# Where K's token term is added: in the copies of M1 and M7 instead of the last addition

## The chip, the core and the metric

The kernel runs on one core of a Trainium2 chip. The metric is the device time of one execution in microseconds; the median of the runs is compared. The engines are named as in the profile: PE is TensorE (matrix products), PEld its weight loads, DVE is VectorE, ACT is ScalarE, POOL is GpSimd and SP is SyncE, which issues most DMAs. SBUF is the working memory of 128 partitions, PSUM the memory into which PE writes, here used as 8 banks of 512 float32 values a partition.

## The reference

Attention over x of shape (8, 512, 512) with 16 heads of 32 columns; one token per batch is projected by the same weights and added to every row of Q and K.

```python
Q = _split_heads(x @ Wq.T + bq)
K = _split_heads(x @ Wk.T + bk)
V = _split_heads(x @ Wv.T + bv)
tQ = _split_heads(tokens @ Wq.T + bq)
tK = _split_heads(tokens @ Wk.T + bk)
cQ = Q + tQ
cK = K + tK
scores = jnp.einsum('bhqd,bhkd->bhqk', cQ, cK) / jnp.sqrt(jnp.float32(HEAD_DIM))
attn = jax.nn.softmax(scores, axis=-1)
out = jnp.einsum('bhqk,bhkd->bhqd', attn, V)
...
x = x + out
```

(The last line stands for the reference's merging of the heads and its addition to x.) Per batch and output column, the token's part of K and both biases are one number: the token term.

## The kernel before

**Groups and thirds.** The 16 heads of a batch make 4 groups of 4 heads (one head to 32 partitions), so there are T = 32 groups t = b * 4 + g. The main loop (`thirds`, line 1156) makes one round for every group and is written by hand as the order of every engine's queue: a manual schedule, in which each engine works through its instructions in the order in which the program issues them and semaphores hold an instruction until its inputs are there and its output is free. A round has three parts, i = 0, 1, 2. In it the row maxima of the scores of the next groups are found (`row_scores` L641 on PE, `one_max` L593 and `row_max_of` L650 on DVE), exponentials are taken (`denominators` L701 and `rest_leaves` L799 on ACT), the weighted sums over V are formed (`times_v_half` L840 on PE), and one piece of the next batch's Q, K or V is projected in each part.

**Projections by seven products.** Q, K and V of a batch are made block-wise in a Strassen-like scheme: for two groups at a time (u = 0 or 1), seven products M1 to M7 of 256 columns replace the block products (`product`, PE at L462). A pair tile holds the upper group (c1 with its second half c12) and the lower group (c2 with its second half c22). For K the work comes in two pieces:

- "k first" (`first_by_others` with `mixed` None): PE makes M1 and M7 into one bank (`one_`), M6 and half of M2 into another (`two_`). DVE copies M1 and M7 to c2 and c22 (L530), adds M1 twice to `two_` to give c1 and c12 (L531), and POOL adds c12 to c22 (L533).
- "k other" (`other_products` with `bias` true): PE makes M4, M5, the other half of M2 and M3 into two banks. DVE adds M5 to c12 (L555), then forms c2 from the bank, c22 and the token term of the lower group (`plus`, L487, group 1), then c1 from the bank, c1 and the token term of the upper group (`plus`, L487, group 0).

Over the run k first and k other occur 14 times each in the main loop, k first in part 2 of every second round and k other in part 1 of the rounds between. Q's "other" goes through the same L487; V has no token term. The first batch's groups take other paths (`project_qk`, `first_products`, and `other_products` with `bias` false).

**The token terms.** `tok` (line 926) holds one float32 per partition for Q or K, group and batch; Q's entries are written by DVE and K's by POOL (`condition_end`, L949), near the start. `bias2` holds twice the biases that go into it.

**Banks.** The eight PSUM banks are handed around by `begin`, `released` and `banks`. After k first the banks of the products go last into the next round's row maxima; after k other the next part's row scores (L641) write into them as well. So PE's L641 waits for the DVE instruction that has read such a bank last.

**The kept exponentials.** Half of a group's exponentials are kept, turned by DVE (`turn_kept`, L660) and swapped between partitions by DMAs issued by SP and POOL (`swap_kept`, L682) until the next round's L840 reads them. The other transfers of the loop load x (L172 and L190) and store results (L917). ACT, DVE and POOL never work on two of their instructions out of order.

Of the kernel before, what the change touches and what calls it, by code (L numbers as in the profile page):

```python
# [9 lines left out]
F32 = mybir.dt.float32  # L10
BF16 = mybir.dt.bfloat16
AF = mybir.ActivationFunctionType
ALU = mybir.AluOpType
# [4 lines left out]
def kernel(  # L18
# [38 lines left out]
    nc = tc.nc  # L57
    P = 128
    B, S, D = x.shape
# [14 lines left out]
    const = ctx.enter_context(tc.tile_pool(name="const", bufs=1))  # L74
# [41 lines left out]
    def banks(i, n=1):  # L116

        row = row_of[0] or [at_end[j] for j in TURNS[turn[0]]]
        j = row[i]
        if n == 1:  # L120
            return psum[:, j, :]
        k = row[i + 1]
        return psum[:, j : k + 1 : k - j, :]
# [273 lines left out]
    def pair_of(t, n):  # L397

        if (n, t // 2) not in pairs:
            pairs[n, t // 2] = qkp.tile([P, 2, S], F32, tag=n, name=f"{n}T_{t // 2}")  # L400
        return pairs[n, t // 2]

    def project_qk_part(t, n, cc, pt, at=slice(0, S)):
        b, g = divmod(t, G)
        nc.tensor.matmul(
            pt[:, at],
            wT[n][:, cc, g * P : (g + 1) * P],
            xT[b][:, cc, at],
            start=(cc == 0),
            stop=(cc == NC - 1),  # L410
        )

    def project_qk_end(t, n, pt):
        b, g = divmod(t, G)
        o = pair_of(t, n)[:, t % 2, :]
        add = tok[:, "qk".index(n), g, b : b + 1]
        if n == "q":
            nc.vector.tensor_scalar(o, pt, add, None, ALU.add)
        else:
            nc.scalar.activation(o, pt, AF.Identity, bias=add)  # L420
        qkT[n, t] = o
# [30 lines left out]
    def product(n, b, u, i, pt, kcs=(0, 1)):  # L452

        for kc in kcs:
            w = block_of_w(n, i, u, kc)
            if n == "v":
                still, moving = block_of_x(b, i, kc, slice(u * P, (u + 1) * P)), w
            else:
                still, moving = w, block_of_x(b, i, kc, slice(0, HS))
            for j in range(HG):  # L460
                r = slice(j * HD, (j + 1) * HD)
                nc.tensor.matmul(  # L462
                    pt[r], still[:, r], moving, start=(kc == kcs[0]), stop=(kc == kcs[-1])
                )

    def twice(a):
        return a.unsqueeze(1).broadcast_to([P, 2, HS])

    def halves(a):
        return a.rearrange("p (h s) -> p h s", h=2)  # L470


    def parts_of(n, b, u):

        if n == "v":
            v = vs[b % 2]
            return v[:, u::2, :HS], v[:, u + 2, :HS], v[:, u::2, HS:], v[:, u + 2, HS:]
        o = pair_of(b * G + u * 2, n)
        return halves(o[:, 0, :]), o[:, 0, HS:], halves(o[:, 1, :]), o[:, 1, HS:]

    def plus(n, b, u, g, o, pt, rest):

        if n == "v":
            nc.vector.tensor_tensor(o, pt, rest, ALU.add)
        else:
            add = tok[:, "qk".index(n), u * 2 + g, b : b + 1]
            nc.vector.scalar_tensor_tensor(o, pt, add, rest, ALU.add, ALU.add)  # L487
# [22 lines left out]
    def first_by_others(n, b, u, dens, at, last, mixed):  # L510

        one_, two_ = halves(banks(at[0])), halves(banks(at[1]))
        c1, c12, c2, c22 = parts_of(n, b, u)
        product(n, b, u, 1, one_[:, 0])
        product(n, b, u, 7, one_[:, 1])
        product(n, b, u, 6, two_[:, 1])
        product(n, b, u, 2, two_[:, 0], (0,))
        if mixed:
            dens((0, 1))
            nc.scalar.copy(c2, one_)  # L520
            dens((2, 3))
            nc.vector.tensor_tensor(c1, two_, twice(c2[:, 0, :]), ALU.add)
            last()
        else:
            dens((0, 1))
            if mixed is False:
                dens((2, 3))
            if mixed is None:
                dens((2, 3))
                nc.vector.tensor_copy(c2, one_)  # L530
                nc.vector.tensor_tensor(c1, two_, twice(c2[:, 0, :]), ALU.add)  # L531
                last()
                nc.gpsimd.tensor_tensor(c22, c22, c12, ALU.add)  # L533
                return
            else:
                nc.scalar.copy(c2, one_)
                nc.scalar.copy(c1, two_)
            last()
            nc.gpsimd.tensor_tensor(c12, c12, c2[:, 0, :], ALU.add)
            nc.gpsimd.tensor_tensor(c22, c22, c12, ALU.add)  # L540
            nc.gpsimd.tensor_tensor(c1[:, 0, :], c1[:, 0, :], c2[:, 0, :], ALU.add)
            return
        nc.gpsimd.tensor_tensor(c22, c22, c12, ALU.add)

    def other_products(n, b, u, dens, small, at, bias=False):

        dens()
        one_, two_ = banks(at[0]), banks(at[1])
        product(n, b, u, 4, one_[:, :HS])
        product(n, b, u, 5, one_[:, HS:])  # L550
        small()
        product(n, b, u, 2, two_[:, :HS], (1,))
        product(n, b, u, 3, two_[:, HS:])
        c1, c12, c2, c22 = parts_of(n, b, u)
        nc.vector.tensor_tensor(c12, one_[:, HS:], c12, ALU.add)  # L555
        if bias and n != "v":
            plus(n, b, u, 1, c2, halves(one_), twice(c22))
        else:
            nc.vector.tensor_tensor(c2, halves(one_), twice(c22), ALU.add)
        plus(n, b, u, 0, c1, halves(two_), c1)  # L560
        if n != "v":
            for g in range(2):
                qkT[n, b * G + u * 2 + g] = pair_of(b * G + u * 2, n)[:, g, :]
# [361 lines left out]

    tok = const.tile([P, 2, NC, B], F32, tag="tok", name="tok")

    part = {}

    def condition(n, pt):  # L930
# [62 lines left out]
    def turn_w(n, ccs, rows=slice(0, D)):  # L993
        for cc in ccs:
            nc.vector.transpose(wT[n][:, cc, rows], ws[n][:, cc, rows])
# [8 lines left out]
    condition_end("k", bank(0), nc.gpsimd)  # L1004
    project_qk_end(0, "k", pk)
    turn_w("v", [0])
    for cc in range(2, NC):
        project_qk_part(1, "q", cc, bank(7))
    project_qk_end(1, "q", bank(7))
# [16 lines left out]
    advance()  # L1026
    row_max(0, 2)
    other_products("q", 0, 1, lambda: denominators(0, 2), nothing, (0, 1))
    advance()
    row_max(0, 3)  # L1030
# [5 lines left out]
    row_max(1, 0)  # L1036
    transpose_max(0, banks(1), nc.scalar.copy)
    other_products("k", 0, 1, lambda: denominators(1, 0), nothing, (0, 2))
    turn_x(NC + 1)
    load_blocks()  # L1040
# [44 lines left out]
    row_max(1, 2)  # L1085
    denominators(1, 2)
    other_products("v", 0, 0, nothing, nothing, (0, 2))
    turn_x(NC + 3)
    load_blocks()
# [32 lines left out]
    def products(b, n, u, product, alone, dens, last, plain):  # L1122

        if product == "first":
            first_by_others(n, b, u, dens, (4, 5) if alone else (0, 1), last, plain)
        else:
            at = (4, 5) if alone else (0, 3)
            if n == "v" and not plain:
                other_by_others(n, b, u, dens, nothing, at)
            else:  # L1130
                other_products(n, b, u, dens, nothing, at, True)
            last()
        if alone:
            released(6, 7, 0, 1, 2, 3, 4, 5)
        elif product == "first":
            released(2, 3, 4, 5, 6, 7, 0, 1)
        else:
            released(1, 2, 4, 5, 6, 7, 0, 3)
# [118 lines left out]
    def one_item(b, n, u, product, at, dens, last):  # L1257

        if n == "v" and product == "first":
            first_of_v(b, u, at)  # L1260
        elif product == "first":
            first_by_others(n, b, u, dens, at, last, False)
        elif n == "v":
            other_by_others(n, b, u, dens, nothing, at)
        else:
            other_products(n, b, u, dens, nothing, at, True)
# [182 lines left out]
    b, g = divmod(t, G)  # L1449
# [52 lines left out]
```

## Time and profile before

| | us |
|---|---|
| median of 3 runs | 650.33 |
| the runs | 650.48, 650.33, 649.67 |
| span of the profiled execution, first to last instruction | 648.4 |
| DVE, kept exponentials turned (L660), 116 instructions | 138.9 |
| DVE, L487 for K at 512 columns, 29 instructions | 21.5 |
| DVE, L531, 14 instructions | 9.7 |
| DVE, L530, 14 instructions | 9.5 |

The profiled execution is known by its span; the medians of the runs lie 1.9 us above it. A timeline row gives the start, the time that the merged instructions took from the first start to the last end, the engine, the line, the operation, output<-inputs, the count, and in brackets how long the engine was idle before and what is taken to have ended that. A row of a single line gives the least, median and greatest duration in ns, and the first and last start. PE's matmuls overlap, so a matmul's duration is no measure of the pace. DVE's instructions overlap as well: the next may start before the recorded end of the last.

### The profile page before, as it was taken

How to read it: one execution, taken by the hardware profiler on the slowest of the kernel's cores; microseconds unless marked ns; L12 is line 12 of the kernel's file. 1: busy time of each engine (PE TensorE's matmuls, PEld its weight loads, DVE VectorE, ACT ScalarE, POOL GpSimd, SP SyncE). 2: the span in 40 equal slices, each digit the busy share in tenths (PEclk: the TensorE clock that was granted, in tenths of full speed). 3: DMA queues.
4: the chain of work that ended last, by engine and by line, in shares of the span. 5: the costliest groups of instructions: out<-in, count | busy, mean ns of one | idle time of the engine just before them, and what ended most of it. 6: DMA issues, size and time to landing. Idle time of an engine off the chain costs nothing. (4 is left out here: it accounts for less than half of the span.)

```text
span 648.4 us, 24814 instructions
## 1 busy us (share of the span) xinstructions
PE 641.6 (99%) x9856; PEld 356.7 (55%) x9856; DVE 600.1 (93%) x845; ACT 533.9 (82%) x1364; POOL 410.6 (63%) x651
## 2 busy tenths in 40 slices
PE   9999999999999999999999999999999999999997
PEld 8445555556555555555555555555555555555531
DVE  3799999999999999999999999999999999999887
ACT  2479888889888989888888988898988888898564
POOL 3633655686665776758567776558766576665650
PEclk9999999999999999999999999999999999999999
DMA  7615688878888788977888978788888767797921
GB/s 191 107 27 84 131 164 172 168 169 191 168 171 174 158 182 177 200 156 153 181 178 170 201 154 186 161 175 169 179 193 162 153 144 164 153 188 155 199 48 34
DMA packets 248457, 102.02 MB, mean 157 GB/s; under 512 B 229962, under 2 KB 230474, under 8 KB 248340
## 3 DMA queue, kind: packets, MB, share of 16 engines
q1 hardware_dynamic: 234196, 65.54, 53.6%
q0 software_dynamic: 12384, 33.83, 20.2%
q8 instruction: 78, 1.28, 0.8%
q10 hardware_dynamic: 1760, 1.05, 0.5%
q14 instruction: 39, 0.32, 0.1%
HBM read 19.75 MB, written 8.39 MB: 43 GB/s over the span
## 5 line engine op out<-in xcount | busy, mean ns | idle before, releaser
L593 DVE TENSOR_REDUCE nmax<-psum 128x1 f32<-128x512 f32 x279 | 177.5, 675 | 9.3 <-PE psum L641 4.9
L701 ACT ACTIVATE psum<-psum,nmax 128x512 f32<-128x512 f32 x248 | 165.3, 678 | 3.6 <-DVE nmax L593 3.0
L641 PE MATMUL psum<-kT,qT 32*128 32x512 f32 x1024 | 162.0, 612 | 0.0
L701 ACT ACTIVATE store<-psum,nmax 128x512 f32<-128x512 f32 x204 | 139.6, 701 | 24.9 <-DVE nmax L593 24.7
L682 POOL DMA_DIRECT2D store<-store x258 | 129.0, 504 | 48.9 <-DMA store<-store 31.8
L799 ACT ACTIVATE store<-psum 128x512 f32<-128x512 f32 x232 | 119.8, 602 | 33.2 <-PE psum L785 33.2
L660 DVE STREAM_TRANSPOSE store<-store 128x1024 f32<-128x1024 f32 x116 | 138.9, 1217 | 0.0
L650 DVE TENSOR_REDUCE nmax<-psum 128x2 f32<-128x1024 f32 x98 | 118.8, 1212 | 0.0
L840 PE MATMUL psum<-store,v 128*32 128x256 f32 x1856 | 106.8, 381 | 0.9 <-DMA store<-store 0.9
L840 PEld LDWEIGHTS psum<-store,v 128*32 128x32 f32 x1856 | 57.2, 110 | 57.9 <-ACT wT_q L632 21.2
L913 POOL TENSOR_TENSOR res<-res,recs 128x512 f32<-128x512 f32 x30 | 31.4, 1046 | 89.0 <-DVE res L912 89.0
L785 PE MATMUL psum<-qT,kT 32*128 32x256 f32 x928 | 83.8, 374 | 0.0
L641 PEld LDWEIGHTS psum<-kT,qT 32*128 32x128 f32 x1024 | 61.5, 183 | 35.4 <-issue 17.8
L785 PEld LDWEIGHTS psum<-qT,kT 32*128 32x128 f32 x928 | 60.8, 184 | 5.9 <-issue 0.3
L701 ACT ACTIVATION_READ_ACCUMULATOR psum<-psum,nmax 128x1 f32 x248 | 55.0, 222 | 0.0
L203 POOL TENSOR_TENSOR xr<-xr,bvs 128x512 f32<-128x512 f32 x30 | 38.6, 1285 | 16.4 <-DMA xr<-in_x_dram 15.7
L462 PE MATMUL psum<-wc_v,xc 128*32 128x256 f32 x768 | 47.7, 379 | 0.0
L462 PE MATMUL psum<-xc,wc_q 128*32 128x256 f32 x720 | 44.7, 379 | 0.0
L462 PE MATMUL psum<-xc,wc_k 128*32 128x256 f32 x720 | 44.5, 379 | 0.0
L701 ACT ACTIVATION_READ_ACCUMULATOR store<-psum,nmax 128x1 f32 x204 | 44.3, 217 | 0.0
L914 POOL TENSOR_TENSOR res<-res,xr 128x512 f32<-128x512 f32 x30 | 38.3, 1278 | 2.3
L462 PE MATMUL psum<-xT,wT_k 128*32 128x256 f32 x480 | 34.5, 382 | 0.0
(191 smaller groups left out, 972.4 us busy)
## 6 DMA issues: line engine op xcount, KB each, us to landing
store<-store SPq DMA_DIRECT2D x264, 128.0 KB, 2.7
store<-store POOLq DMA_DIRECT2D x258, 128.0 KB, 3.8
out_dram<-res SPq DMA_DIRECT2D x122, 64.0 KB, 3.7
xr<-in_x_dram SPq DMA_DIRECT2D x120, 64.0 KB, 4.2
x<-in_x_dram SPq DMA_DIRECT2D x112, 64.0 KB, 3.3
w_q<-in_L_cond_Wq_dram SPq DMA_DIRECT2D x4, 256.0 KB, 3.9
w_v<-in_L_cond_Wv_dram SPq DMA_DIRECT2D x16, 64.0 KB, 2.5
w_k<-in_L_cond_Wk_dram SPq DMA_DIRECT2D x16, 48.0 KB, 2.7
```

The lines of the kernel that those rows point to most:

```text
L203: nc.gpsimd.tensor_tensor(xr[t], xr[t], bias, ALU.add)
L462: nc.tensor.matmul(pt[r], still[:, r], moving, start=(kc == kcs[0]), stop=(kc == kcs[-1]))
L593: nc.vector.tensor_reduce(nmax[t][:, qc, j : j + 1, 0], pt, AX.X, ALU.max, negate=True)
L641: nc.tensor.matmul(pt, qkT["q", t][r, qc * P : (qc + 1) * P], qkT["k", t][r, :], start=True, stop=True,)
L650: nc.vector.tensor_reduce(nmax[t][:, qc, pr * 2 : pr * 2 + 2, 0], pt, AX.X, ALU.max, negate=True)
L660: nc.vector.transpose(e, e)
L682: (nc.gpsimd if here else nc.sync).dma_start(to, of)
L701: nc.scalar.activation(to, of, AF.Exp, bias=nmax[t][:, qc, j, :], accum_out=sums[t][:, qc, j, :],)
L785: nc.tensor.matmul(banks(j)[:, i * HS : (i + 1) * HS], qkT["k", t][r, kc * P : (kc + 1) * P], qkT["q", t][r, KQ * P :], start=False, stop= ...
L799: nc.scalar.activation(e[:, j], banks(j), AF.Exp)
L840: nc.tensor.matmul(pt[j * HD : (j + 1) * HD, half * HS : (half + 1) * HS], vs[b % 2][:, kc, (g * HG + j) * HD : (g * HG + j + 1) * HD], e, ...
L914: nc.gpsimd.tensor_tensor(y, y, xr.pop(t), ALU.add)
```

## The change

K's upper token term is added to M1 and M7 while they are copied. Then c1, c12 and c22 carry it: c1 and c12 once, c22 twice, since M7 and M1 both have it. In the second piece c1 needs no term any more and becomes a plain addition; c2, which adds c22, gets the lower term less twice the upper one. These numbers are put into a new table `tok_left` of 2 x 8 float32 a partition (u and batch), made by one DVE instruction near the start, behind the first transpose of W_v. Q, V and the first batch keep what they had.

```diff
@@ first_by_others
             if mixed is None:
                 dens((2, 3))
-                nc.vector.tensor_copy(c2, one_)
+                add = tok[:, "qk".index(n), u * 2, b : b + 1]
+                nc.vector.tensor_scalar(c2, one_, add, None, ALU.add)
                 nc.vector.tensor_tensor(c1, two_, twice(c2[:, 0, :]), ALU.add)
                 last()
                 nc.gpsimd.tensor_tensor(c22, c22, c12, ALU.add)
@@ other_products
         nc.vector.tensor_tensor(c12, one_[:, HS:], c12, ALU.add)
-        if bias and n != "v":
-            plus(n, b, u, 1, c2, halves(one_), twice(c22))
+        if bias and n == "k":
+            add = tok_left[:, u, b : b + 1]
+            nc.vector.scalar_tensor_tensor(
+                c2, halves(one_), add, twice(c22), ALU.add, ALU.add
+            )
+            nc.vector.tensor_tensor(c1, halves(two_), c1, ALU.add)
         else:
-            nc.vector.tensor_tensor(c2, halves(one_), twice(c22), ALU.add)
-        plus(n, b, u, 0, c1, halves(two_), c1)
+            if bias:
+                plus(n, b, u, 1, c2, halves(one_), twice(c22))
+            else:
+                nc.vector.tensor_tensor(c2, halves(one_), twice(c22), ALU.add)
+            plus(n, b, u, 0, c1, halves(two_), c1)
@@ behind the definition of tok
+    tok_left = const.tile([P, 2, B], F32, tag="tok_left", name="tok_left")
+
+    def bias_left():
+        nc.vector.scalar_tensor_tensor(
+            tok_left, tok[:, 1, ::2, :], -2.0, tok[:, 1, 1::2, :], ALU.mult, ALU.add
+        )
@@ start
     project_qk_end(0, "k", pk)
     turn_w("v", [0])
+    bias_left()
     for cc in range(2, NC):
         project_qk_part(1, "q", cc, bank(7))
     project_qk_end(1, "q", bank(7))
```

## The prediction

> **What bounds the kernel now.** I read the page first, then the busy time of each engine in one stretch that is a round of the main loop (a third, 19.15 us), then the timeline, engine by engine, of the stretches in which the edited lines run.
>
> ```profile
> PE 641.6 (99%) x9856; PEld 356.7 (55%) x9856; DVE 600.1 (93%) x845; ACT 533.9 (82%) x1364; POOL 410.6 (63%) x651
> 161.96:181.11 19.15, 19.15 (x316) 10.74 (x317) 18.35 (x26) 16.88 (x45) 13.09 (x22) 1.00 0.82 169
> ```
>
> The columns of the stretch are length, then busy time of PE, PEld, DVE, ACT, POOL, the granted clock and the DMA share. TensorE never pauses by this account, VectorE is busy 18.35 of 19.15 us, and the clock is full. The two take turns in holding each other: VectorE waits for a product in PSUM, and TensorE waits until VectorE has emptied a bank. So a shorter VectorE instruction is worth something only where TensorE waits for its end, and a longer one costs only there. All depends on which of the two edited places is such a gate.
>
> K's other half ("k other", in every second third, 14 times) looks like this:
>
> ```profile
> 174.50 0.74 DVE L487 SCALAR_TENSOR_TENSOR kT<-psum,tok,kT 128x512 f32<-128x512 f32 x1
> 175.41 0.75 DVE L487 SCALAR_TENSOR_TENSOR kT<-psum,tok,kT 128x512 f32<-128x512 f32 x1 [0.17 <-PE psum L462]
> 176.08 1.23 DVE L660 STREAM_TRANSPOSE store<-store 128x1024 f32<-128x1024 f32 x1
> ...
> 174.24 1.05 PE L462 MATMUL psum<-xT,wc_k 128*32 128x256 f32 x16
> 175.45 1.03 PE L785 MATMUL psum<-qT,kT 32*128 32x256 f32 x16
> 176.31 1.14 PE L641 MATMUL psum<-kT,qT 32*128 32x512 f32 x8
> 177.38 0.42 PE L462 MATMUL psum<-wT_v,xc 128*32 128x256 f32 x4
> ...
> 176.28 0.34 PEld L641 LDWEIGHTS psum<-kT,qT 32*128 32x128 f32 x8 [0.20 <-ACT psum L701]
> ```
>
> The first L487 writes c2, the second c1. TensorE ends product 3 at 174.24 + 1.05 = 175.29; c1 starts 0.12 later, so TensorE sets its start. c1 ends at 175.41 + 0.75 = 176.16, and the weight load of the next row scores (L641) comes 0.12 behind that. The row names ScalarE for this pause, but a third in which c1 stands differently to TensorE tells them apart:
>
> ```profile
> 98.20 1.40 DVE L487 SCALAR_TENSOR_TENSOR kT<-psum,tok,kT 128x512 f32<-128x512 f32 x2
> 98.79 1.03 PE L785 MATMUL psum<-qT,kT 32*128 32x256 f32 x16
> 99.72 0.34 PEld L641 LDWEIGHTS psum<-kT,qT 32*128 32x128 f32 x8 [0.30 <-ACT psum L701]
> ```
>
> Here c1 ends at 98.20 + 1.40 = 99.60, the load follows at 99.72, again 0.12 behind c1, while the distance to the end of L785 is 99.72 - 99.82 = -0.10 here and 176.28 - 176.48 = -0.20 there. The load follows c1. The scores write the bank that c1 empties, so this is a true gate. What it costs shows against Q's other half, in which the scores are not held up:
>
> ```profile
> 157.65 1.03 PE L641 MATMUL psum<-kT,qT 32*128 32x512 f32 x8
> 158.60 1.07 PE L462 MATMUL psum<-xT,wT_k 128*32 128x256 f32 x16
> ...
> L641 PE MATMUL psum<-kT,qT x1024: 585/587/692, 22.9 to 625.1; 32*128 32x512 f32 x171
> ```
>
> From scores to products it is 158.60 - 157.65 = 0.95 us for Q and 177.38 - 176.31 = 1.07 for K: 0.12 us lost, in the place where the longest score matmul takes 692 instead of 587 ns.
>
> **The change part by part.** (1) c1 of k other becomes a tensor_tensor. The durations stand in the views of single lines (least, median and greatest ns):
>
> ```profile
> L531 DVE TENSOR_TENSOR kT<-psum,kT x14: 690/692/693, 85.3 to 583.4; 128x512 f32<-128x512 f32 x14
> L530 DVE COPY kT<-psum x14: 678/678/680, 84.4 to 582.4; 128x512 f32<-128x512 f32 x14
> L320 DVE TENSOR_SCALAR wT_q<-psum x2: 690/690/691, 12.1 to 14.6; 128x512 f32<-128x512 f32 x2
> L418 DVE TENSOR_SCALAR qT<-psum,tok x2: 751/751/751, 19.5 to 23.0; 128x512 f32<-128x512 f32 x2
> ```
>
> The old c1 takes 0.75; the same addition without the token term 0.692 (L531). I take that, as its operands are the same: c1 ends 0.750 - 0.692 = 0.058 us sooner. The shortest row of this size from PSUM is the copy with 678, so 73 ns is the most. The gate has 105 ns (692 - 587) to give, so all of it can pass. 14 x 0.058 = 0.81 us; bounds 0 (if something else holds the load just behind) and 14 x 0.073 = 1.0.
>
> [...]
>
> Does the gain survive behind the gate? From the gated scores to the next wait of VectorE:
>
> ```profile
> 177.44 1.29 DVE L593 TENSOR_REDUCE nmax<-psum 128x1 f32<-128x512 f32 x2
> 181.11 0.69 DVE L1238 TENSOR_TENSOR v<-psum,v 128x512 f32<-128x512 f32 x1 [0.20 <-PE psum L462]
> ...
> 179.99 1.05 PE L462 MATMUL psum<-wc_v,xT 128*32 128x256 f32 x16
> 182.92 1.29 PE L840 MATMUL psum<-store,v 128*32 128x256 f32 x20
> ```
>
> TensorE goes from the scores through the products (177.38 to 179.99 + 1.05 = 181.04) without a pause, and VectorE waits 0.20 us for the last of them at L1238. So what TensorE wins, VectorE gets, and the next third begins sooner. That VectorE itself is done with c1 earlier is worth nothing extra: between L660 (176.08 + 1.23 = 177.31) and L593 it waits 0.13 us for those scores.
>
> (2) The copy of M1 and M7 (L530) becomes a tensor_scalar with a column of tok. Nearest rows: 690 with a number (L320), 751 with tok (L418). I take 751, as it has the same operands: +73 ns on 678, bounds 0 and +73. Where it stands:
>
> ```profile
> 161.04 0.68 DVE L530 COPY kT<-psum 128x512 f32<-128x512 f32 x1
> 161.96 0.69 DVE L531 TENSOR_TENSOR kT<-psum,kT 128x512 f32<-128x512 f32 x1 [0.24 <-ACT store L701]
> 161.22 0.61 PE L462 MATMUL psum<-xT,wT_k 128*32 128x256 f32 x8
> 162.70 0.30 PEld L641 LDWEIGHTS psum<-kT,qT 32*128 32x128 f32 x7 [0.22 <-DVE kT L531]
> ...
> 18.92 0.29 DVE L943 TENSOR_REDUCE sum_q<-psum 128x32 f32<-128x128 f32 x1 [0.75 <-PE psum L921]
> 19.24 0.19 DVE L949 TENSOR_TENSOR tok<-sum_q,bias 128x32 f32<-128x32 f32 x1
> ```
>
> L531 needs M1 from L530 and the second product's bank from TensorE. L530 ends at 161.72, the bank at 161.22 + 0.61 = 161.83, and L531 starts 0.13 after the bank, the distance that c1 has to its product. A wait of VectorE for itself is much shorter: L949 starts 0.03 after the L943 that it reads (19.21 to 19.24). So TensorE holds L531, and L530 has 161.83 - 161.72 = 0.11 us of cover; it uses 0.073. Cost nothing. With the cover gone it would be 14 x 0.073 = 1.0 us, since L531 is a gate too: the scores' load at 162.70 follows its end at 162.65.
>
> (3) c2 of k other reads tok_left in the place of tok, in the same form: 0. (4) The table itself is one VectorE instruction on 16 elements a partition, queued between a transpose of W_v and L418:
>
> ```profile
> 21.54 0.70 DVE L995 STREAM_TRANSPOSE wT_v<-w_v 128x512 f32<-128x512 f32 x1
> 21.70 0.24 POOL L949 TENSOR_TENSOR tok<-sum_k,bias 128x32 f32<-128x32 f32 x1 [6.10 <-DVE sum_k L943]
> 23.05 0.75 DVE L418 TENSOR_SCALAR qT<-psum,tok 128x512 f32<-128x512 f32 x1 [0.81 <-PE psum L405]
> ```
>
> Its input is there at 21.94, VectorE is free at 22.24, and L418 waits for TensorE until 23.05. Something like L949's 0.19 to 0.24 us fits into the 0.81 of waiting. Without that cover it would be 0.2 us, once. No DMA is added or moved, and no queue of SP or POOL is passed.
>
> **The sum.** The span of 648.4 less 0.81 is 647.6. The median of the runs, 650.33, is 1.9 above the span; with that put back, 649.5.
>
> **The rivals.** Rival 1, no change (650.3): c1 ends sooner, but the load at 176.28 is then held by something next in line, or ScalarE becomes the limit. For it: the row names ScalarE's L701; against it: the constant 0.12 behind c1. It is also the case in which the two forms of c1 cost alike; 0.74 to 0.75 us in the rows of L487 against 690 to 693 ns of L531 speak against that.
>
> Rival 2, the tensor_scalar pushes L531: the 0.24 idle before L531 would be the delay of its own wait for L530, not TensorE. Then 14 x 0.073 = 1.0 us is added on a gate, and with the 0.81 won the time is 650.33 + 1.0 - 0.81 = 650.5. It decides from 0.11 us of extra length on, if the reading above is right; against it stands the 0.03 of L949.
>
> Rival 3, slower by the layout: the new tile takes 64 bytes a partition and stands ahead of everything allocated after it, the buffers of all transfers among them. If transfers get longer by that, the swaps of the kept exponentials come late for L840. Their cover:
>
> ```profile
> 177.26 0.49 POOL L682 DMA_DIRECT2D store<-store  x1 [0.16 <-issue]
> DMA to landing us min/median/max: 2.2/3.5/6.3
> ```
>
> The last swap issued at 177.26 lands at 180.8 by the median and 183.6 at worst; the second half of L840's matmuls, which reads it, starts some 1.75 us behind 182.92. So there are 1.1 to 3.9 us of cover, and landings would have to grow by a third of 3.5 us before a late one costs anything. If they did, and 26 thirds lost 0.1 us each, it would be 649.5 + 2.6 = 652.1. [...]
>
> **How the numbers follow.** The forecast has 0.55, rival 1 0.2, rival 2 0.1, rival 3 0.1, and 0.05 is left for a larger gain than I can account for. About 0.2% (1.3 us) is what a measurement of this kernel can tell from no change; the runs shown spread over 0.8 us. The forecast's -0.13% lies inside that, with some chance to fall beyond it: a third of its 0.55, and the rest for larger gains, make 0.25 for faster. Rival 3 and a part of rival 2 make 0.13 for slower, and 0.62 is left for no change. The range takes in the forecast with both bounds of (1), both rivals without a layout effect, the scatter of the runs, and the 1.0 us of (2) on top of no gain (651.4): 648.6 to 651.6.
>
> **What would show it.** Right: the new c1 at 0.69 us, L641's load behind it still 0.12 behind its end, the stretch from scores to products in k other at 1.01 instead of 1.07, the longest score matmul nearer to 587; L530 at 0.75 with L531 still 0.13 behind TensorE's product and the idle before it down from 0.24 to about 0.17; two thirds together shorter by 0.06 us. Wrong: a start of L531 that moves with L530's end (rival 2), a load of L641 that stays where it is when c1 ends earlier (rival 1), waits of L840 or POOL for DMA that grow (rival 3), or a tensor_scalar beyond 0.79 us.

## The result and the profile after

| | median, us | least to greatest, us | runs |
| --- | --- | --- | --- |
| before | 650.33 | 649.67 to 651.34 | 12 |
| with the change | 654.50 | 651.18 to 658.99 | 12 |

The ratio is 1.0069 (95% interval 1.0049 to 1.0088): the change costs 0.7%, where 649.5 us was forecast. The changed kernel also scatters over 7.8 us, the old one over 1.7. Its profiled execution is a long one, 657.93 us with a span of 656.1, so its losses are read for where they are; how large they are on the whole, the medians say. (What the prediction calls a third, 19.15 us, is one whole round of the main loop.)

Line numbers have moved. The copies of M1 and M7 are now L531, the addition behind them L532 (was L531), c2 and c1 L559 and L562 (were L487), row scores L649 (L641), the results' write L925 (L917), the swaps of exponentials L690 (L682), the splitting of the maxima L723 to L726 (L715 to L718), their transposing DMA L735 (L727), the maxima into PSUM L780 (L772), the sums over V L848 (L840).

First the edited places, in the timeline of the changed kernel: the first piece of K, then the other piece (start, duration, engine, line).

```profile
160.80 0.74 DVE L531 TENSOR_SCALAR kT<-psum,tok 128x512 f32<-128x512 f32 x1
161.72 0.69 DVE L532 TENSOR_TENSOR kT<-psum,kT 128x512 f32<-128x512 f32 x1 [0.17 <-ACT store L709]
160.98 0.61 PE L462 MATMUL psum<-xT,wT_k 128*32 128x256 f32 x8
...
174.27 0.74 DVE L559 SCALAR_TENSOR_TENSOR kT<-psum,tok_left,kT 128x512 f32<-128x512 f32 x1
175.18 0.69 DVE L562 TENSOR_TENSOR kT<-psum,kT 128x512 f32<-128x512 f32 x1 [0.17 <-PE psum L462]
174.01 1.05 PE L462 MATMUL psum<-xT,wc_k 128*32 128x256 f32 x16
176.08 1.08 PE L649 MATMUL psum<-kT,qT 32*128 32x512 f32 x8
177.09 0.42 PE L462 MATMUL psum<-wT_v,xc 128*32 128x256 f32 x4
...
175.99 0.34 PEld L649 LDWEIGHTS psum<-kT,qT 32*128 32x128 f32 x8
```

At the edited places all is as forecast. The new copy takes 0.74 us and ends at 161.54; the product that L532 needs ends later, at 160.98 + 0.61 = 161.59, and L532 starts 0.13 behind that. The plain c1 takes 0.69, ends at 175.87, and the scores' weight load follows 0.12 behind it. From scores to products it is now 177.09 - 176.08 = 1.01 us, where it was 1.07.

Then the waits, by engine, line and what ended them (us in all, times, longest). Before, for the transfers:

```profile
POOL store L682 <- DMA store<-store: 31.8, 30, 2.4
PE psum L840 <- DMA store<-store: 0.9, 1, 0.9
```

and with the change:

```profile
POOL store L690 <- DMA store<-store: 60.3, 52, 3.1
PEld L780 <- DMA maxT<-split: 5.6, 4, 1.5
PE psum L780 <- DMA maxT<-split: 3.7, 4, 1.0
PE psum L848 <- DMA store<-store: 2.8, 1, 2.8
```

POOL, which issues 258 of the 522 swaps and waits for earlier ones, waits twice as long for them (60.3 us instead of 31.8). Waits of two kinds stop PE, which is what counts: four for the transposed maxima, which PE never waited for before, and one for a swap, which takes 2.8 us in place of 0.9.

How such a wait for the maxima comes about shows in one round. POOL, SP and PE before:

```profile
176.61 0.49 POOL L682 DMA_DIRECT2D store<-store  x1 [0.87 <-DMA store<-store]
177.26 0.49 POOL L682 DMA_DIRECT2D store<-store  x1 [0.16 <-issue]
177.75 0.27 POOL L715 CAST split<-nmax 128x16 bf16<-128x16 f32 x1
...
174.38 4.07 SPq L917 DMA_DIRECT2D out_dram<-res  x4
178.50 3.33 SPq L172 DMA_DIRECT2D x<-in_x_dram  x4
181.93 1.21 SPq L727 DMA_TRANSPOSE maxT<-split  x1
...
189.60 0.40 PE L772 MATMUL psum<-maxT,onesb 3*128 3x512 bf16 x4
```

and the same round with the change:

```profile
176.99 0.49 POOL L690 DMA_DIRECT2D store<-store  x1 [0.17 <-issue]
178.47 1.00 POOL L690 DMA_DIRECT2D store<-store  x2 [0.99 <-DMA store<-store]
179.47 0.27 POOL L723 CAST split<-nmax 128x16 bf16<-128x16 f32 x1
...
180.45 0.27 POOL L726 TENSOR_TENSOR split<-rest,split 128x16 bf16<-128x16 f32 x1
...
176.10 4.61 SPq L925 DMA_DIRECT2D out_dram<-res  x4
180.75 3.31 SPq L172 DMA_DIRECT2D x<-in_x_dram  x4
184.17 1.21 SPq L735 DMA_TRANSPOSE maxT<-split  x1
...
188.76 0.61 PE L462 MATMUL psum<-xT,wT_q 128*32 128x256 f32 x8
190.39 0.40 PE L780 MATMUL psum<-maxT,onesb 3*128 3x512 bf16 x4 [1.02 <-DMA maxT<-split]
```

POOL waits 0.99 us for a swap before its last two, so the split of the maxima starts at 179.47 instead of 177.75. That is not what holds the transposing DMA: the split is complete at 180.45 + 0.27 = 180.72, and SP is still busy until 180.75 + 3.31 = 184.06 with the results' write and x's load, which stand ahead of it in SP's queue. The transposing DMA goes out right behind them, at 184.17 instead of 181.93. It then lands at 190.35, 6.18 us after its issue (2.70 in the same round of before, where it landed at 184.63), and PE, ready since 189.37, starts 0.04 behind the landing. So the landing is 2.24 us later by SP's queue and 3.48 by the transfer, 5.72 in all, where before it came 4.97 ahead of PE's use at 189.60. The other three waits look alike: in all four the split is complete 2.1 to 3.3 us before x's load leaves SP, and the transposing DMA follows that load by 0.11. Why SP is late and the transfer long, the rows don't tell. Over all 29 such DMAs (view of that line, before and then after):

```profile
DMA to landing us min/median/max: 2.5/2.9/4.5
```

```profile
DMA to landing us min/median/max: 2.4/4.1/6.8
```

The rounds themselves, worked out as the distances of the first L840 (L848) matmuls of the first 28 groups, read:

```
             first at   rounds over 19.5 us                     first to last   last to end of span
before         87.1     none (19.10, 19.15 or 19.17 mostly)        517.3            44.0
after          87.1     20.19, 20.19, 19.98, 19.68, 20.03          521.1            47.9
```

So an undisturbed round is 0.05 us shorter or equal, five are 0.6 to 1.1 us longer, and the loop as a whole loses 3.8 us. The other 3.9 of the span's 7.7 are lost behind the loop. There PE waits 2.77 us for a swap, and the stretches that follow (length, then busy time of PE, PEld, DVE, ACT, POOL, the granted clock, the DMA share, GB/s) run at a lower clock:

```profile
624.17 2.50 PE L848 MATMUL psum<-store,v 128*32 128x256 f32 x32 [2.77 <-DMA store<-store]
```

```profile
624.00:626.60 2.60, 2.43 (x40) 1.75 (x40) 0.00 (x0) 0.00 (x0) 1.07 (x1) 0.77 0.67 104
626.60:629.20 2.60, 2.60 (x26) 1.82 (x23) 1.31 (x3) 0.64 (x3) 1.04 (x1) 0.57 0.00 0
629.20:634.00 4.80, 4.80 (x48) 1.46 (x43) 4.08 (x6) 4.17 (x9) 3.59 (x3) 1.00 0.34 52
```

The wait is 1.84 us longer than the 0.93 at the same place before, and the clock of 0.77 and 0.57 costs, as an estimate from these stretches, 2.6 x (0.23 + 0.43) = 1.7 us more: 3.6 of the 3.9. How much of this is the change's doing is not shown. This wait differs from execution to execution: in the profiles of the experiments below it is 0.55 us with 128 idle bytes, 0.99 with the table at the end, 1.22 with 64 idle bytes, and 2.12 where x, q and k move by 64 bytes and the results and the store by 128. Before, the clock stayed at 1.00 there:

```profile
618.53 1.93 PE L840 MATMUL psum<-store,v 128*32 128x256 f32 x32 [0.93 <-DMA store<-store]
```

```profile
618.50:620.40 1.90, 1.87 (x40) 1.43 (x40) 0.83 (x1) 0.26 (x1) 1.90 (x2) 1.00 0.02 4
620.40:623.00 2.60, 2.60 (x36) 1.34 (x31) 2.00 (x5) 1.70 (x5) 1.37 (x2) 1.00 0.59 101
```

The change adds no transfer: both profiles have 248457 packets. What it does to transfers is to move buffers: `tok_left` takes 64 bytes a partition and is allocated ahead of x, q and k, the residuals, the results, the transposed maxima and the store of exponentials. In the built program the store and the results began at multiples of 256 bytes and x and the residuals 128 above one; with the change each stands 64 higher, and the pieces of 128 bytes, in which x, residuals and results travel, then lie across multiples of 256 in every second case (and of 128 in every case).

### The profile page after: what moved, and what is told of

Its sections match the earlier page's. It is cut to its first block, busy times and chain, and to the rows that moved or that the text cites. A ratio compares the mean times of both kernels' runs of the same rounds, so it can differ in the third digit from the quotient of the medians.

```text
span 656.1 us, 24815 instructions
## 1 busy us (share of the span) xinstructions
PE 643.0 (98%) x9856; PEld 358.0 (55%) x9856; DVE 602.3 (92%) x846; ACT 534.0 (81%) x1364; POOL 410.3 (63%) x651
## 2 busy tenths in 40 slices
DMA packets 248457, 102.02 MB, mean 155 GB/s; under 512 B 229962, under 2 KB 230474, under 8 KB 248340
## 5 line engine op out<-in xcount | busy, mean ns | idle before, releaser
L690 POOL DMA_DIRECT2D store<-store x258 | 129.1, 503 | 83.3 <-DMA store<-store 60.3
L649 PE MATMUL psum<-kT,qT 32*128 32x512 f32 x1024 | 162.3, 611 | 0.0
L848 PE MATMUL psum<-store,v 128*32 128x256 f32 x1856 | 107.6, 382 | 3.1 <-DMA store<-store 2.8
L848 PEld LDWEIGHTS psum<-store,v 128*32 128x32 f32 x1856 | 57.5, 110 | 60.3 <-ACT wT_q L640 21.2
L649 PEld LDWEIGHTS psum<-kT,qT 32*128 32x128 f32 x1024 | 61.3, 184 | 35.4 <-issue 17.9
```

The source lines that it names most:

```text
L649: nc.tensor.matmul(pt, qkT["q", t][r, qc * P : (qc + 1) * P], qkT["k", t][r, :], start=True, stop=True,)
L690: (nc.gpsimd if here else nc.sync).dma_start(to, of)
L848: nc.tensor.matmul(pt[j * HD : (j + 1) * HD, half * HS : (half + 1) * HS], vs[b % 2][:, kc, (g * HG + j) * HD : (g * HG + j + 1) * HD], e, ...
```

## The experiments

The theory: the instructions of the change win what was forecast, and the 64-byte shift loses more. Its rival: the longer copy or the new order of VectorE's work makes something late, and the DMA waits only follow. Each kernel was timed in turn with the kernel before on one chip, and the ratio is to that.

**1. The layout alone, and the change without it.** To the kernel before, an unused tile of 64 bytes in the place where the table was put:

```diff
     tok = const.tile([P, 2, NC, B], F32, tag="tok", name="tok")
+    pad = const.tile([P, 16], F32, tag="pad", name="pad")
```

> The kernel before with an unused tile of 64 bytes a partition at the place of the new table, so that every buffer behind it lies 64 bytes further, as in the changed kernel; the instructions are those of before. Theory A (the layout makes the transfers longer, the transposed maxima land late): 652 to 656 us, runs as scattered as those of the changed kernel, waits of PE for maxT as there. Theory B (the new pace of TensorE and VectorE makes transfers collide; the layout is innocent): 650.3 within 0.5, no wait for maxT.

Measured: 653.11 us (652.49 to 657.08), ratio 1.0054 (1.0034 to 1.0073), 2.7 us more at the medians and 3.5 by the ratio. The waits, with every instruction as before:

```profile
POOL store L682 <- DMA store<-store: 67.5, 52, 4.7
PEld L772 <- DMA maxT<-split: 4.5, 4, 1.5
PE psum L772 <- DMA maxT<-split: 2.5, 4, 1.0
PE psum L840 <- issue: 1.1, 1, 1.1
PE psum L840 <- DMA out_dram<-res: 0.9, 1, 0.9
```

A tile that nothing reads or writes makes a loss of this kind and the same new wait. Two more pauses of about 1 us stand at L840, in the loop at 456.45 and 476.93 us; the row gives the last release that the trace shows, so what L840 waited for there is not certain.

The other way round, the whole change with its table behind the store:

```diff
-    tok_left = const.tile([P, 2, B], F32, tag="tok_left", name="tok_left")
+    tok_left = EB.tile([P, 2, B], F32, tag="tok_left", name="tok_left")
```

> The changed kernel with the new table placed behind the last tile, so that no other tile moves; the computation is that of the change. Theory A: the loss is gone and the 0.8 us of the gate remain, 649.2 to 649.8 us, waits for maxT gone. Theory B: as the changed kernel, 652 to 656 us.

Measured: 649.47 us (649.10 to 650.59), ratio 0.9987 (0.9978 to 0.9996). The profiled span is 647.6, the one the prediction's sum gave; its rounds are 19.10 and 19.17, from first to last 516.4 us, 0.9 less than before. PE waits for no maxima, and POOL's wait is back:

```profile
POOL store L690 <- DMA store<-store: 29.7, 30, 2.5
```

The two together show the cause: the shift of the buffers loses, and the instructions of the change win.

**2. The gain by itself.** Only c1 of K becomes plain; K's upper token term is left out there, and nothing is moved.

```diff
-        plus(n, b, u, 0, c1, halves(two_), c1)
+        if bias and n == "k":
+            nc.vector.tensor_tensor(c1, halves(two_), c1, ALU.add)
+        else:
+            plus(n, b, u, 0, c1, halves(two_), c1)
```

> The kernel before with K's last addition plain and nothing else changed (K's upper token term is left out in the main loop). It has the shorter gate without a longer copy of M1 and M7, a new table or a new layout. Theory A: 649.2 to 649.8 us. Theory B: over 651 us, since the pace of TensorE is the same as in the changed kernel.

Measured: 649.68 us (648.96 to 650.42), ratio 0.9991 (0.9982 to 1.0000), span 648.0. That is 0.7 us at the median, near the 0.81 forecast, though the interval reaches 1. The longer copy, which this kernel lacks and experiment 1's second kernel has, costs nothing that can be seen (649.47 against 649.68).

**3. Is it the size of the shift?** The same idle tile with 128 bytes, on the kernel before, and later the change itself with 64 bytes of padding behind its table, so that all moves by 128:

```diff
     tok = const.tile([P, 2, NC, B], F32, tag="tok", name="tok")
+    pad = const.tile([P, 32], F32, tag="pad", name="pad")
```

> The kernel before with an unused tile of 128 bytes a partition there. It asks which shift hurts. Theory A in the form that a piece of 128 bytes must not straddle a boundary of 256: no piece does so with this shift either, 650.3 within 0.5. Theory A in the form that the start of the 4 KB swaps must be a multiple of 256: 652 to 656 as with 64 bytes. Theory B: 650.3 within 0.5.

```diff
     tok_left = const.tile([P, 2, B], F32, tag="tok_left", name="tok_left")
+    const.tile([P, 16], F32, tag="pad", name="pad")
```

> The changed kernel with its table widened to 128 bytes a partition, so that all buffers behind it move by 128 and none straddles. Theory A: the loss is gone, 649.3 to 650.0 us. If the table's place itself or its extra instruction cost anything: over 651 us.

Measured: 650.54 us (650.18 to 653.73), ratio 1.0010 (1.0000 to 1.0020) for the idle tile, with POOL's waits as before:

```profile
POOL store L682 <- DMA store<-store: 33.0, 33, 2.3
```

And 649.56 us (649.11 to 652.09), ratio 0.9988 (0.9979 to 0.9996) for the padded change, 1.0 us faster than before. A shift by 128 bytes harms little or nothing (0.2 us at the medians of the idle tile, where 64 bytes cost 2.7), so it is not that buffers move, nor their order, but by how much: 64 bytes put the pieces of 128 across multiples of 256, 128 bytes don't. Whether 256 is the multiple that counts is not shown, since 64 bytes put them across multiples of 128 as well, and no other shift was run.

**4. Which buffer?** Idle tiles of 64 bytes that move some buffers by 64 and the rest by nothing or by 128. First the store alone, then the results, residuals, transposed maxima and small tiles (the store by 128; later expectations call this one e6), then x with q and k (e7):

```diff
     EB = ctx.enter_context(tc.tile_pool(name="eb", bufs=1))
+    EB.tile([P, 16], F32, tag="pad_eb", name="pad_eb")
```

> The kernel before with 64 unused bytes a partition directly ahead of the store of the exponentials, so that only the store moves by 64 (the pieces of 4 KB that the swaps move start 64 behind a multiple of 256). If the swaps are what the layout makes slower: 652 to 656 us. If it is the transfers in pieces of 128 bytes: 650.3 within 0.5.

```diff
     op = ctx.enter_context(tc.tile_pool(name="op", bufs=2))
+    op.tile([P, 16], F32, tag="pad_op", name="pad_op", bufs=1)
...
     EB = ctx.enter_context(tc.tile_pool(name="eb", bufs=1))
+    EB.tile([P, 16], F32, tag="pad_eb", name="pad_eb")
```

> The kernel before with 64 unused bytes ahead of the buffers of residuals, results and transposed maxima, and 64 more behind them, so that these lie 64 further and the store 128 further, which did no harm. Residuals and results go in pieces of 128 bytes, of which every second one then straddles a multiple of 256. If these pieces are the cause: 652 to 656 us. If the swaps are: 650.3 within 0.5.

```diff
     xp = ctx.enter_context(tc.tile_pool(name="xp", bufs=2))
+    xp.tile([P, 16], F32, tag="pad_xp", name="pad_xp", bufs=1)
...
     op = ctx.enter_context(tc.tile_pool(name="op", bufs=2))
+    op.tile([P, 16], F32, tag="pad_op", name="pad_op", bufs=1)
```

> The kernel before with 64 unused bytes ahead of the buffers of x and 64 more behind Q and K, so that only x (and Q and K, which no DMA touches) lie 64 further, all behind them 128. x is written in pieces of 128 bytes. If writes into SBUF that straddle are the cause, as much per transfer as in the residuals: 651 to 653 us. If reads (results) or the swaps are: 650.3 within 0.5.

| what is moved by 64 bytes | median, us | ratio (95% interval) |
| --- | --- | --- |
| store of exponentials | 651.19 | 1.0008 (0.9997 to 1.0019) |
| results, residuals, transposed maxima | 652.59 | 1.0032 (1.0022 to 1.0042) |
| x, q and k | 650.84 | 1.0008 (0.9999 to 1.0017) |

Only the second is clear of no change. The store's 0.9 us at the medians comes near it: all its runs (650.72 to 651.77) lie above the median of before, 650.33, and the interval is widened by a single run of before at 653.52. Its 651.19 and the 650.84 of x lie between the times that were expected for the two theories, so they decide for neither. Only the second kernel's profile has the long waits of POOL and a wait for the maxima, the latter of the weight loads alone:

```profile
POOL store L684 <- DMA store<-store: 54.6, 44, 4.2
PEld L774 <- DMA maxT<-split: 1.4, 3, 0.6
```

With x, q and k moved, the profile shows the long wait behind the loop that was mentioned above, at a full clock:

```profile
PE psum L842 <- DMA store<-store: 2.1, 1, 2.1
```

That group was then taken apart. A helper sets an idle tile of 64 bytes into the pool `op` before the first tile of a name is made, once ahead of what is to move and once, where needed, behind it:

```diff
+        pad(0)
         y = op.tile([P, NB, BL], F32, tag="res", name=f"res_{t}")
```

> The kernel before with 64 unused bytes ahead of the results' buffers and 64 more behind them: only the results (read from SBUF by the stores, in pieces of 128 bytes) lie 64 further, the store of the exponentials 128. If the straddling reads of the results carry most of the 2.3 us of e6: 652 to 653 us. If the residuals or the transposed maxima do: 650.4 within 0.4.

```diff
+                pad(0)
                 xr[t] = op.tile([P, NB, BL], F32, tag="xr", name=f"xr_{t}")
...
+        pad(1)
         apart = op.tile([P, HG, NS, NS], F32, tag="apart", name=f"apart_{t}")
```

> The same with the pads around the residuals' buffers: only the residuals (written into SBUF in pieces of 128 bytes) lie 64 further, what is behind them 128. If writes that straddle cost as in e7 (0.5 us for x): 650.8 to 651.2 us. If they carry most of the 2.3 us: 652 to 653 us.

```diff
+        pad(0)
         maxT[t] = op.tile([P, S], BF16, tag="maxT", name=f"maxT_{t}")
...
+                pad(1)
                 xr[t] = op.tile([P, NB, BL], F32, tag="xr", name=f"xr_{t}")
```

> The same with the pads around the transposed maxima (1 KB a partition, written by the transposing DMA that TensorE waits for): only these lie 64 further, what is behind them 128. If a misplaced transpose is itself slow and so late: 652 to 653 us. If it is only late because it queues behind the other transfers: 650.4 within 0.4.

| moved by 64 bytes | median, us | ratio (95% interval) |
| --- | --- | --- |
| results | 651.65 | 1.0013 (1.0004 to 1.0022) |
| residuals | 650.70 | 1.0002 (0.9993 to 1.0011) |
| transposed maxima | 650.59 | 1.0001 (0.9992 to 1.0009) |

Of the single buffers the results alone are clear of no change, by 1.1 us at the medians. That is hardly more than the store's 0.9, and 651.65 lies between the times expected for the two theories, so the results are not shown to carry most of the loss. In their profile the loop takes 517.3 us, as before, and PE waits for no maxima; what that execution loses lies behind the loop (44.9 us instead of 44.0). So waits for the maxima are seen only where the results and other buffers move by 64 together. The results are read from SBUF and written to the output in pieces of 128 bytes; the residuals are written into SBUF in the same pieces and cost no time that can be seen (650.70 us against 650.57). The mean time of a packet of 128 bytes on the queue of all three, worked out from the traces, goes with it:

```
before                         12.93 ns     results moved        13.24 ns
with the change                13.61 ns     residuals moved      13.01 ns
idle tile of 64 bytes          13.87 ns     x, q, k moved        12.92 ns
idle tile of 128 bytes         12.91 ns     store moved          12.92 ns
change with table at the end   12.92 ns     padded change        12.90 ns
results, residuals, maxima     13.35 ns     maxima moved         12.94 ns
```

Packets lengthen clearly only where the results are moved by 64 bytes, and more where other buffers are moved with them; with the residuals alone it is 13.01, a little above the 12.90 to 12.94 of the rest. The times don't add up: results, residuals and maxima moved one by one lose 1.1, 0.1 and 0.0 us, together 2.3. That the losses are waits that arise only once several transfers are late at the same time would fit, but no run shows it.

**5. Is it the queues behind the swaps?** If the transposing DMA is late because POOL holds the split back behind a waiting swap, splitting and transposing ahead of POOL's swaps should give the loss back. Done on the changed kernel, and on the kernel before as a control:

```diff
                 first = range(6 if t + 1 < KEPT[-1] else 3)
-                swap_kept(t, 2, first)
                 split_max(t + 1)
                 turn_max(t + 1)
+                swap_kept(t, 2, first)
```

> The changed kernel, layout and all, but in part 1 of every round the maxima are split and their transpose is issued ahead of the third move of the swaps, not behind it. If the lost time is that the transposes stand behind swaps which end late: no wait of TensorE for the transposed maxima is left and the time falls from 654.5 to 650 to 652 us. If the slower transfers cost by another way (the swaps themselves late for L840, residuals late for POOL): 653 us or more, and the waits move there.

> The kernel before with that order: the control. 650.3 within 0.7, as no transpose is waited for there; more if the swaps that now go later come late for L840.

Measured: 658.83 us (654.53 to 664.11), ratio 1.0135 (1.0102 to 1.0169) for the changed kernel, and 656.14 us (654.02 to 657.88), ratio 1.0094 (1.0080 to 1.0107) for the control. The waits of the changed kernel in the new order:

```profile
PE psum L848 <- DMA store<-store: 2.9, 3, 1.8
PE psum L780 <- DMA maxT<-split: 2.1, 1, 2.1
POOL store L690 <- DMA store<-store: 8.0, 11, 2.2
```

and of the control:

```profile
PE psum L840 <- DMA store<-store: 1.9, 2, 1.5
PE psum L840 <- issue: 1.7, 1, 1.7
```

The experiment misses its aim. POOL's waits for swaps do go (60.3 to 8.0 us), but the order itself costs 6 us without any shift, and in both kernels PE now waits at the sums over V inside the loop, by most rows for a swap; the control's longest wait in the loop, 1.7 us, is put down to "issue", which names nothing. With the change PE also waits once for the maxima, 2.1 us, with no wait of POOL for a swap ahead of the split: the split is complete at 310.99, and the transposing DMA goes out at 319.95, 0.11 behind x's load on SP. That is what the changed kernel's four waits showed: SP's queue, and not the split on POOL, holds the transposing DMA back. How SP comes to be late, and why the transfer takes longer (6.18 us instead of 2.70 in the round shown), is not settled.

**6. A faster kernel.** K's token term adds the same vector tK to every row of K, and with it cQ . tK to all scores of a query, which softmax cancels. Leaving it out everywhere leaves the attention as it is, and then both pieces of K can be plain and no table is needed:

```diff
-            nc.scalar.activation(o, pt, AF.Identity, bias=add)
+            nc.scalar.copy(o, pt)
...
-        if n == "v":
+        if n != "q":
             nc.vector.tensor_tensor(o, pt, rest, ALU.add)
...
-    condition("k", bank(5))
-    condition_end("k", bank(0), nc.gpsimd)
```

> The kernel before with K's token term left out everywhere, its computation at the start too (a vector added to all rows of K adds the same number to all scores of a row, which the softmax takes away again); the layout is that of before. Both theories of the layout expect the 0.8 us of the gate; the start may give up to 1.5 us more, as ScalarE waits 1.4 us there for K's term and TensorE for ScalarE: 648.0 to 649.6 us. If the gate were no gate: 650.3 less what the start gives.

Measured: 648.13 us (647.64 to 650.05), ratio 0.9969 (0.9958 to 0.9981), span 646.2. It beats both kernels: 2.2 us below before, 6.4 below the change as it was made. In its trace the first L840 begins at 85.8 us instead of 87.1, which is 1.3 us won at the start, and from first to last the rounds take 516.4 instead of 517.3, which is the gate's 0.9.

## Why the prediction was wrong

**Step (1), the gate: right.** The load of the scores kept its 0.12 behind c1, the stretch from scores to products is 1.01 as named, and the gain of 0.81 was measured as 0.9 (table at the end), 1.0 (padded change) and 0.7 (c1 alone). (The copy with 678 ns was not the shortest row of this size from PSUM: the plain addition L559 of before takes 672 at its shortest, by which the upper bound of the gain would be 1.1 us.) Rival 1, no change, falls with it: the interval of the first two excludes it. One sign was read from too wide a row. The line's greatest score matmul stays at 692 ns (table at the end), since matmuls of 692 stand in other places too, as at 161.76; at the gate itself it fell by the 0.05 us won, as the same eight score matmuls show, before and with the table at the end (least, median and greatest ns):

```profile
L641 PE MATMUL psum<-kT,qT x8: 587/624/692, 176.3 to 176.9; 32*128 32x512 f32 x8
L649 PE MATMUL psum<-kT,qT x8: 587/594/639, 176.2 to 176.6; 32*128 32x512 f32 x8
```

**Step (2), the copy behind TensorE's product: right.** The term was +73 ns (751); the least, median and greatest of 14 are

```profile
L531 DVE TENSOR_SCALAR kT<-psum,tok x14: 739/741/743, 84.3 to 586.3; 128x512 f32<-128x512 f32 x14
```

so +63, inside the cover of 0.11. The idle time before L532 went from 0.24 to 0.17, as named, and its start still follows the product by 0.13. Rival 2 falls.

**Steps (3) and (4): right as to their instructions.** c2 keeps its 0.74, and the first L848 begins at 87.1 in both traces, so the start pays nothing for the table's instruction.

**What failed: the table's place was left out of the sum.** Step (4) priced the table as one hidden instruction and "No DMA is added or moved" closed the account. No DMA is, but the buffers of nearly all DMAs are, and that term, set to 0 in the sum, measured +0.54% (0.34 to 0.73), about 3.5 us (2.7 at the medians), against a gain of 0.8. The prediction had it as rival 3 and gave it 0.1.

**Why rival 3 came out too small.** Its cover was worked out for one reader, L840: 1.1 to 3.9 us between the last swap's landing and its use, so that landings would have to grow by a third. In the loop of the changed kernel that nearly holds: one wait of 0.4 us at L848 (at 360.02; the idle tile's loop has two of about 1 us at L840). What came late in the loop was a transfer that the prediction did not look at, the transposed maxima. It had a cover too, and a larger one than the swap's: 4.97 us in the round shown, from its landing at 184.63 to PE's use at 189.60. The step that failed was to ask only how much one transfer must grow. The transposing DMA stands in SP's queue behind writes and loads, so it inherits their delay (2.24 us) and adds its own (2.70 grew to 6.18), and the sum of 5.72 exceeds the cover. At the median its landing went from 2.9 to 4.1 us, and PE lost 3.7 us in four waits for it. The waits of POOL for DMA, named as the sign of rival 3, did grow, from 31.8 to 60.3 us, though POOL's split is not what held these four back. Behind the loop a swap came late for L848, as rival 3 has it, at the one place where PE waited 0.93 us for it already, so without any cover; that row was not looked for, but as this wait reaches 2.1 us in another layout, its 2.77 us are not shown to be the shift's. The price, 26 rounds at 0.1 us, had the wrong shape: a few rounds lose about 1 us each, and not the same ones in the two shifted kernels (the changed one's waits at 190, 248, 345 and 423 us, the idle tile's larger ones at 364, 456, 477 and 483); a time made of a few such losses would scatter, which fits the 651.2 to 659.0 us.

**What stays open.** The changed kernel (654.5) is not below the idle tile (653.1), though it should be by the 0.8 won. Their ranges overlap widely (651.18 to 658.99 and 652.49 to 657.08), and the two have not been timed in turn often enough to say. For the late maxima, POOL's split is ruled out in the four waits of the changed kernel; why SP's queue runs late and why the transfer lengthens, by so much more than the mean packet does, stays open. So does which buffers beside the results are needed for the loss.

## What to carry to other kernels

A new tile, however small, is an edit to the address of every buffer allocated after it: put it last (649.47 us here), or pad it so that what stands behind it moves by a step that the runs show to be harmless (128 bytes here, 649.56 us, where 64 idle bytes alone cost 2.7 us), and price its place before its instruction. When transfers may get longer, work out the cover not of their reader alone but of everything that waits in a queue behind them, add up the delays along that queue (here 2.24 and 3.48 us against a cover of 4.97), and look first for the places where the critical engine already waits for one. Before a term is moved to a cheaper place, ask whether the result needs it at all.

## What the runs showed of the hardware

In these traces reads of 128-byte pieces from SBUF cost more when their buffer is moved by 64 bytes: 13.24 instead of 12.93 ns a packet over the whole queue with only the results moved, and 13.87 with everything moved; a move of 128 bytes gives 12.91. With the results moved the mean packet is longer by 2%. As 63488 of the 198144 packets are the results' (124 writes of 64 KB), that is an estimated 1 ns or 8% on each of these, if all of it falls on them; buffers that are written show less (13.01 ns with the residuals moved, 12.92 with x, q and k).

PE's granted clock fell to 0.50 after a long wait, for 3.41 us, in two places. In the changed kernel PE was idle for 2.77 us at L848 (to 624.17), and the granted clock is 0.50 from 625.40 to 628.81; the averages of 0.77 and 0.57 above come from that, and it cost an estimated 1.7 us. In the changed kernel of experiment 5 PE was idle for 2.14 us (to 327.13), and the clock is 0.50 from 327.47 to 330.88; the mean clock of both executions is 0.997. The weight loads paused for longer than PE, 3.57 us in the first case and 2.62 in the second; the first is

```profile
624.14 1.64 PEld L848 LDWEIGHTS psum<-store,v 128*32 128x32 f32 x32 [3.57 <-issue]
```

But 2.12 us of idle time with x, q and k moved left the clock at 1.00; nor did waits of 1.02 us in the loop of the changed kernel lower it:

```profile
190.30:192.90 2.60, 2.51 (x37) 1.86 (x40) 1.68 (x4) 1.13 (x3) 2.36 (x4) 1.00 1.33 172
```

In these traces the length of one wait alone does not decide. That shows behind PE's last product, after which PE stays idle: before, it ends at 643.96 + 0.77 = 644.73 and the clock is 0.50 from 645.79, 1.06 us later; with the change it ends at 651.23 + 0.77 = 652.00 and the clock stays at 1.00 until 656.12, 4.12 us later. What decides, and what sets the 3.41 us, is not shown.
